# Layer 2 of a four-layer model: the gated branch's last batch placed beside the collecting of the experts' rows

## The chip, the core and the metric

The kernel runs on one core of a Trainium2 chip. The metric is the device time of one execution in microseconds (us), lower is better. The engines of the core are PE (matrix products and transposes), DVE (vector work), ACT (activations and copies), POOL (here it issues the indirect transfers) and SP (it issues the plain transfers). Each engine works through its own queue in order, and they meet through semaphores. A "window" below is a stretch of the profiled span, and "clock" is the share of full speed that the throttle granted to PE.

## What is computed

The model has four layers on `x` of 4 batches of 1024 tokens of 128 numbers (float32). Every layer takes a layer norm of `x` and adds two branches of it to `x`. Only layer 2 and its borders matter here:

```python
xn = _layernorm(x)
x  = x + _L2_attn_ref(xn, ...) + _L2_ffn_ref(xn, ...)

# _L2_attn_ref: the gated branch, for each batch by itself; S=128, E=256
xn   = x / max(norm(x) * D**-0.5, EPS) * g
uv   = silu(xn @ uv_w.T);  u, v, base = uv[:E], uv[E:2E], uv[2E:]   # along the last axis
q, k = rope(base * gamma + beta)
kern = square(relu((q @ k.T + w_rel[idx]) / sqrt(S)))
out  = x * res_scale + (u * (kern @ v)) @ o_w.T

# _L2_ffn_ref: eight experts, top 2 of each token, 640 rows for an expert
probs      = softmax(xf @ router_w.T);  topw, topi = top_k(probs, 2)
# tokens sorted by expert and by falling weight; those ranked past 640 are dropped
eo         = (silu(disp @ wg) * (disp @ wu)) @ wd                   # disp: the rows of each expert
out[token] += eo[expert, rank] * weight
```

## The kernel before

`x` and `xn` lie on chip as 128 channels by 4096 tokens, in eight tiles of 512 tokens (`NT`, `W`). Layer 2 (`_layer2`, L1736) has three stages.

**Stage A** runs two generators against each other under an order written out by hand (`manual_schedule` for PE, DVE, ACT and POOL): the routing (`_dispatch`) and the gated branch (`_gated`, L1568). `_layer2` takes one step of the routing after each step of the gated branch, and two after each of the first eight. Whatever a generator issues between two of its `yield`s stands together in the engines' queues.

The routing turns `xn` to rows of tokens, `xtok` (four PE transposes L909 and an ACT copy L910 for each of the eight tiles), computes the logits (L918, 32 products into the PSUM tile `lg`), softmax and top two on DVE (L930 to L965), and then finds for each expert the weight of its 640th heaviest token: `_heaviest` searches it bit by bit from bit 29 to 0. For a bit DVE counts (L868), PE sums the counts over partitions (L873), DVE sets the bit and the next candidate (L874 to L877). Ranks, slots and addresses follow (to L992), and then POOL issues 64 scatters (L1000), each of 128 token rows of `xtok` into the experts' buffer `buf` in memory. They all write one buffer, and each waits for the one before.

The gated branch runs over four batches. For a batch `project` normalises (L1611, L1612), makes `u`, base and `v` (L1621, L1634, activations on ACT) and turns the base (`gy`, L1649, L1657, L1660 on DVE). Then, for two halves of the queries and eight blocks of keys, `score` makes a product (L1666, near the diagonal one more, L1670), ACT adds the relative weight (L1672), DVE squares (L1674, `gkern`), and `weigh` (L1681) multiplies by `v` into the accumulator `gacc`, two products for a block. After eight blocks DVE multiplies by `u` (L1690), and `close` (L1695, L1700, L1701) projects back and adds to `x`. The scores of the next half, and the projection of the next batch (`ahead`), are issued between the weighings. A float32 product of 512 columns shows as two matmuls in the profile.

**Stage B** (`_experts`, L1007): SP loads an expert's weights (L1020 to L1022) and its rows from `buf` (L1027), PE and the others compute, SP stores the outcome to `res`.

**Stage C** takes `_collect` and `_norm_beside` by turns (`_together`), in an order that the scheduler chooses. `_collect` has, for each of the eight tiles, eight gathers by POOL (L1081, 128 rows each), DVE's weighing of the rows (`cl_y`, L1089, L1091), four PE transposes (L1092, into the PSUM tile `cl_tp`), and an addition to `x` (L1094). Six row buffers of each kind let the gathers run ahead. `_norm_beside` is the layer norm of layer 3 behind it: centring (L286, L287, ACT square L289), variance (L306 to L312) one tile behind, scaling (ACT L317, PE L320, DVE L321) two tiles behind. The first products of layer 3 (convolutions L1793, activations L1801, stores of rows to memory L1802, betas L1814 and L1815) follow and use `xn` as its tiles come out; the last of those four stores, for batch 3, is used below as the end of stage C.

Layer 0 uses `_dispatch` without the search, and `_collect` beside its shared expert (`_shared`, L1112 to L1117).

Of the kernel before, what the change touches and what calls it, by code (L numbers as in the profile page):

```python
# [11 lines left out]
F32 = mybir.dt.float32  # L12
# [6 lines left out]
PSUM = bass.MemoryType.PSUM  # L19
DRAM = bass.MemoryType.DRAM  # L20

P = 128
B, L, D = 4, 1024, 128
T = B * L
W = 512
NT = T // W
# [263 lines left out]
    return sq  # L290


def _norm_beside(k, whole):


    nc, tc = k.nc, k.tc
    with tc.tile_pool(name="nb", bufs=3) as w, tc.tile_pool(
        name="nb_ps", bufs=2 if whole else 1, space=PSUM
    ) as misc:
        squares = {}  # L300

        def variance(t):
            st = misc.tile([P, W], F32, name="misc")
            sq, own = squares.pop(t), slice(4 * t, 4 * t + 4)
            for i in range(4):
                nc.tensor.matmul(  # L306
                    st[:, i : i + 1], sq[:, i * P : (i + 1) * P], k.mean[:, 0:1], start=True, stop=True
                )
            nc.vector.tensor_copy(k.var[:, own], st[:, :4])
            if whole:  # L310
                nc.scalar.activation(k.inv[:, own], k.var[:, own], AF.Sqrt, bias=k.eps5)
                nc.vector.reciprocal(k.inv[:, own], k.inv[:, own])  # L312

        def scale(t):
            c = slice(t * W, (t + 1) * W)
            spread = w.tile([P, 4, P], F32, name="nb_s")
            nc.scalar.copy(spread, _bc(k.inv[:, 4 * t : 4 * t + 4], 2, P))  # L317
            ps = misc.tile([P, W], F32, name="misc")
            for i in range(4):
                nc.tensor.transpose(ps[:, i * P : (i + 1) * P], spread[:, i], k.ident)  # L320
            nc.vector.tensor_tensor(k.xn[:, c], k.xn[:, c], ps, ALU.mult)  # L321

        for t in range(NT + 2):
            if whole and t >= 2:
                scale(t - 2)
            if 1 <= t <= NT:
                variance(t - 1)
            if t < NT:
                squares[t] = _centre(k, t, misc, w)
            if t < NT:  # L330
                yield
# [509 lines left out]
    return a  # L841


def _heaviest(k, weight, pool):


    nc = k.nc
    flat = lambda t: t.rearrange("p t e -> p (t e)")
    by_expert = lambda t: t.rearrange("p t e -> p e t")

    def turned(src):

        ps = k.misc.tile([P, W], F32, name="misc")
        for m in range(2):
            nc.tensor.transpose(ps[:, m * P : (m + 1) * P], src[:, m * P : (m + 1) * P], k.ident)
        return ps[:, : 2 * P]


    row = pool.tile([P, 2 * P], F32, name="bis_row")
    mask = pool.tile([P, 2 * P], F32, name="bis_mask")  # L860
    nc.vector.tensor_copy(row, turned(flat(weight)))
    part = pool.tile([P, 1], F32, name="bis_part")

    thr, cand, on = (pool.tile([P, 1], I32, name="bis_" + n) for n in ("thr", "cand", "on"))
    nc.vector.memset(thr, 0)
    nc.vector.memset(cand, 1 << 29)
    for bit in range(29, -1, -1):
        nc.vector.tensor_scalar(  # L868
            mask, row, cand.bitcast(F32), None, ALU.is_ge, ALU.add, accum_out=part
        )  # L870
        yield
        ps = k.misc.tile([P, W], F32, name="misc")
        nc.tensor.matmul(ps[:, :1], k.same8, part, start=True, stop=True)  # L873
        nc.vector.tensor_scalar(on, ps[:, :1], float(CAP), float(1 << bit), ALU.is_ge, ALU.mult)  # L874
        nc.vector.tensor_tensor(thr, thr, on, ALU.bitwise_or)
        if bit:
            nc.vector.tensor_scalar(cand, thr, 1 << (bit - 1), None, ALU.bitwise_or)  # L877
    equal, above = (pool.tile([P, TT, E], F32, name="bis_" + n) for n in ("equal", "above"))
    for dst, op in ((above, ALU.is_gt), (equal, ALU.is_equal)):
        nc.vector.tensor_scalar(mask, row, thr.bitcast(F32), None, op)  # L880
        yield
        nc.vector.tensor_copy(flat(dst), turned(mask))
    left, n = (pool.tile([P, E], F32, name="bis_" + n) for n in ("left", "n"))
    nc.vector.tensor_reduce(n, by_expert(above), AX.X, ALU.add)
    yield
    ps = k.misc.tile([P, W], F32, name="misc")
    nc.tensor.matmul(ps[:, :E], k.ones, n, start=True, stop=True)
    nc.vector.tensor_scalar(left, ps[:, :E], -1.0, float(CAP), ALU.mult, ALU.add)
    rank = _prefix(k, equal, pool, "bis_rank")
    nc.vector.tensor_tensor(rank, rank, _bc(left, 1, TT), ALU.is_lt)  # L890
    nc.vector.tensor_tensor(equal, equal, rank, ALU.mult)
    nc.vector.tensor_tensor(equal, equal, above, ALU.add)
    return equal


def _dispatch(k, rw, normed, by_weight, den_eps, keep, rows, bufs, banks, got):
# [3 lines left out]
    with tc.tile_pool(name="rt", bufs=1) as r, tc.tile_pool(name="rtw", bufs=2) as w, tc.tile_pool(  # L900
# [1 line left out]
    ) as k.misc, tc.tile_pool(name="rt_lg", bufs=1, space=PSUM) as lp:  # L902

        xtok = rows.tile([P, TT, D], F32, name="xtok")
        for t in range(NT):
            ps = k.misc.tile([P, W], F32, name="misc")
            for i in range(4):
                c = t * W + i * P
                nc.tensor.transpose(ps[:, i * P : (i + 1) * P], k.xn[:, c : c + P], k.ident)  # L909
            nc.scalar.copy(xtok[:, 4 * t : 4 * t + 4, :].rearrange("p t d -> p (t d)"), ps)  # L910
            yield

        lg = lp.tile([P, TT, E], F32, name="lg")
        for t in range(NT):
            c = slice(t * W, (t + 1) * W)
            x = k.xn[:, c]
# [44 lines left out]
        if by_weight:  # L961
            nc.vector.tensor_tensor(pr, hot[0], _bc(top[0], 2, E), ALU.mult)
            nc.vector.tensor_tensor(tmp, hot[1], _bc(top[1], 2, E), ALU.mult)
            nc.vector.tensor_tensor(pr, pr, tmp, ALU.add)
            nc.vector.scalar_tensor_tensor(pr, chosen, -1.0, pr, ALU.add, ALU.add)  # L965
            chosen = yield from _heaviest(k, pr, r)
            yield
            rank = _prefix(k, chosen, r, "rank")
            kept = chosen
        else:  # L970
            rank = _prefix(k, chosen, r, "rank")
            kept = r.tile([P, TT, E], F32, name="kept")
            nc.vector.tensor_scalar(kept, rank, float(CAP), None, ALU.is_lt)
# [95 lines left out]
def _collect(k, got, res, acc, banks):  # L1069


    nc, tc = k.nc, k.tc
    with tc.tile_pool(name="cl", bufs=6) as g, tc.tile_pool(name="cl_ps", bufs=banks, space=PSUM) as ps:
        for t in range(NT):
            tp = ps.tile([P, W], F32, name="cl_tp")
            for i in range(4):
# [56 lines left out]
def _layer0(k, a):  # L1133
    _layer_norm(k)
    with k.tc.tile_pool(name="keep0", bufs=1) as keep:
        rw = k.load(keep, a["l0_rw"])
        with k.tc.tile_pool(name="rows0", bufs=1) as rows:
            got = []
            for _ in _dispatch(k, rw, True, False, 0.0, keep, rows, [k.buf[0]] * 2, 4, got):
                pass  # L1140
            _attention0(k, a)
        _experts(k, a["l0_rg"], a["l0_ru"], a["l0_rd"], k.buf[:1], k.res[0])
        _together(_shared(k, a, k.x), _collect(k, got, k.res[0], k.x, 1), _norm_beside(k, False))

# [418 lines left out]

def _gated(k, a):  # L1568


    nc, tc = k.nc, k.tc
# [1 line left out]
    with ExitStack() as s:  # L1573
# [22 lines left out]
        def project(z):  # L1596
# [18 lines left out]
            for half in range(2):  # L1615
                own = slice(half * W, (half + 1) * W)
                for dst, at in ((base, 512), (z.u, 0)):
                    yield
                    ps = big.tile([P, 2, W], F32, name="big")
                    for m in range(2):  # L1620
                        nc.tensor.matmul(  # L1621
                            ps[:, m, :],
                            uvw[:, at + m * P : at + (m + 1) * P],
# [53 lines left out]
        def weigh(z, half, jc):  # L1677
            if jc == 0:
                z.acc = accs.tile([P, 2, W], F32, name="gacc")
            for e in range(2):  # L1680
                nc.tensor.matmul(  # L1681
                    z.acc[:, e, :],
                    z.v[:, jc, e * P : (e + 1) * P],
# [16 lines left out]
            nc.vector.scalar_tensor_tensor(t, k.xn[:, c], k.vec("l2_rs"), ps, ALU.mult, ALU.add)  # L1700
            nc.vector.tensor_tensor(k.x[:, c], k.x[:, c], t, ALU.add)  # L1701

        zs = [SimpleNamespace(b=b, kern=([], [])) for b in range(B)]
        for _ in project(zs[0]):
            yield
        for jc in range(8):
            yield
            score(zs[0], 0, jc)
        ahead = iter(())
        for n in range(2 * B):  # L1710
            z, half = zs[n // 2], n % 2
            if half == 0 and n // 2 + 1 < B:
                ahead = project(zs[n // 2 + 1])
            for jc in range(8):
                yield
                if n + 1 < 2 * B:
                    if jc == 0 and half == 1:
                        for _ in ahead:
                            pass
# [1 line left out]
                    if half == 0:  # L1721
                        next(ahead, None)
                    yield
                weigh(z, half, jc)
                if jc == 2 and n:
                    close(zs[(n - 1) // 2], (n - 1) % 2)
                if half == 0:
                    next(ahead, None)
                    if jc % 2:
                        next(ahead, None)  # L1730
        yield
        close(zs[-1], 1)
        yield


def _layer2(k, a):  # L1736
    _layer_norm(k)
    with k.tc.tile_pool(name="keep2", bufs=1) as keep:
# [2 lines left out]
        got = []  # L1741
        with k.tc.tile_pool(name="rows2", bufs=1) as rows, k.tc.manual_schedule(engines=ENGINES3):
            routes = _dispatch(k, rw, False, True, 1e-6, keep, rows, k.buf[1:] * 2, 1, got)
            gated = _gated(k, a)
            next(gated)
            for n, _ in enumerate(gated):
                next(routes, None)
# [2 lines left out]
            for _ in routes:  # L1750
                pass
        _experts(k, a["l2_rg"], a["l2_ru"], a["l2_rd"], k.buf[1:], k.res[1])
        _together(_collect(k, got, k.res[1], k.x, 2), _norm_beside(k, True))

# [533 lines left out]
```

## Time and profile before

| | us |
|---|---|
| median of 3 runs (lowest, highest) | 4741.51 (4738.85, 4744.04) |
| the profiled execution | 4741.99 |
| its span | 4740.2 |
| layer 2: last logits end | 3470.27 |
| layer 2: search | 3484.4 to 3560.5 |
| layer 2: scatters, first start and last end | 3581.91, 3747.60 |
| layer 2: rows of the first expert reach PE | 3763.13 |
| layer 2: first gather | 3888.79 |
| layer 3: store of the rows of batch 3 | 3998.10 |

The moments count from the start of the span. The granted clock over the span is 0.859. PE is busy for 83% of the span, DVE for 65%, ACT for 54% and POOL for 14%; such shares are means over stages with different limits, so what bounds layer 2 has to be read in its own windows. In a row of the windows the first figures are the length and then, for each engine, its busy time and its number of instructions. A row of the waits gives the engine and line that waited, what it waited for, the sum, the number and the longest. In the timeline the bracket at the end is the idle time before the instruction and what ended it.

### The profile page before, as it was taken

The numbers are of one execution on the slowest core, as the hardware profiler recorded it, in microseconds if no ns is written. First come the engines' busy times: TensorE is split into PE (matmuls) and PEld (weight loads), VectorE is DVE, ScalarE is ACT, GpSimd is POOL, SyncE is SP. The second block draws the span as 40 slices with busy tenths as digits, with TensorE's granted clock in tenths as the row PEclk, the third lists the DMA queues.
The fourth block names the chain that finished last, engine by engine and source line by source line (L and its number), as shares of the span: only waits on it lengthen the run. The fifth ranks groups of instructions, "written<-read, shape, count | busy, mean of one in ns | idle before, by whom it ended". The sixth has DMA issues, their size and how long they took to land. (4 is left out here: it accounts for less than half of the span.)

```text
span 4740.2 us, 54727 instructions
## 1 busy us (share of the span) xinstructions
PE 3911.8 (83%) x21048; PEld 1791.9 (38%) x21048; DVE 3093.1 (65%) x4481; ACT 2583.1 (54%) x3674; POOL 685.3 (14%) x632
## 2 busy tenths in 40 slices
PE   4679999998968888888886888888879986898675
PEld 3223333364422222222223555555544463343221
DVE  5868989722335655656567888888565323799686
ACT  1257877831249999999993555555422222343332
POOL 2310000003200000000003223233103213000242
PEclk6689999999977777767777999999889997999688
DMA  2411111021221010010002111111100122400001
GB/s 87 119 41 56 29 56 29 11 70 50 15 83 58 18 50 18 27 36 18 18 1 78 34 36 41 36 37 34 51 1 20 52 72 67 109 1 9 0 0 53
DMA packets 107496, 191.83 MB, mean 40 GB/s; under 512 B 23138, under 2 KB 48354, under 8 KB 105378
## 3 DMA queue, kind: packets, MB, share of 16 engines
q1 hardware_dynamic: 98756, 166.31, 12.4%
q0 software_dynamic: 8192, 16.79, 1.7%
q10 hardware_dynamic: 288, 5.24, 0.3%
q8 instruction: 166, 2.72, 0.2%
q14 instruction: 94, 0.77, 0.1%
HBM read 95.00 MB, written 67.39 MB: 34 GB/s over the span
## 5 line engine op out<-in xcount | busy, mean ns | idle before, releaser
L790 DVE TENSOR_TENSOR p<-p,e 128x1024 f32<-128x1024 f32 x512 | 586.4, 1219 | 322.0 <-ACT e L788 322.0
L773 PE MATMUL big<-q,k 32*128 32x512 f32 x2048 | 559.3, 631 | 181.8 <-ACT p L784 76.7
L583 DVE TENSOR_REDUCE m<-mx 128x2 f32<-128x1024 f32 x512 | 620.9, 1223 | 101.2 <-PE mx L575 94.1
L468 PE MATMUL av<-p,v 128*32 128x256 f32 (+1 forms) x5632 | 666.3, 528 | 0.2
L666 ACT ACTIVATE p<-s 128x512 f32<-128x512 f32 x1024 | 551.1, 597 | 187.9 <-PE s L657 174.4
L773 PEld LDWEIGHTS big<-q,k 32*128 32x128 f32 x2048 | 210.0, 228 | 706.4 <-ACT e L788 351.1
L657 PE MATMUL s<-q,k 64*128 64x512 f32 x1024 | 278.6, 496 | 45.7 <-DMA q<-mrows 31.3
L788 ACT ACTIVATE e<-big,neg_mu 128x1024 f32<-128x1024 f32 x256 | 262.2, 1126 | 12.5 <-PE big L773 12.3
L575 PE MATMUL mx<-k,q 64*128 64x512 f32 x1024 | 239.4, 438 | 32.4 <-DVE m L583 17.8
L784 ACT ACTIVATE p<-big,neg_mu 128x1024 f32<-128x1024 f32 x256 | 261.3, 1201 | 2.5 <-PE big L773 2.3
L788 ACT ACTIVATE e<-big 128x1024 f32<-128x1024 f32 x256 | 242.6, 1040 | 27.5 <-PE big L773 25.9
L784 ACT ACTIVATE p<-big 128x1024 f32<-128x1024 f32 x256 | 239.4, 1072 | 8.4 <-PE big L773 8.1
L1227 POOL TENSOR_TENSOR lqk<-lt 128x512 f32<-128x512 f32 x128 | 162.7, 1271 | 516.5 <-DVE lt L1218 450.3
L1081 POOL DMA_INDIRECT cl_row<-res,back x128 | 122.3, 955 | 727.8 <-DMA in_l_su_sb<-in_l_su 473.5
L1200 PE MATMUL lps<-f_wqkv,lh 128*128 128x512 f32 x384 | 215.4, 649 | 11.0 <-DVE lo L1355 6.8
L468 PEld LDWEIGHTS av<-p,v 128*32 128x32 f32 x5632 | 121.3, 111 | 254.8 <-issue 205.2
L657 PEld LDWEIGHTS s<-q,k 64*128 64x128 f32 x1024 | 107.9, 184 | 284.2 <-issue 161.1
L1318 ACT ACTIVATE lsm<-lsm 128x512 f32<-128x512 f32 x128 | 80.6, 630 | 222.0 <-DVE lsm L1317 220.5
L1000 POOL DMA_INDIRECT buf<-xtok,to x128 | 129.0, 1008 | 402.5 <-DMA buf<-xtok,to 222.5
L1193 POOL MEMSET lva<- 128x32 f32 x16 | 2.4, 152 | 1147.0 <-PE av L468 1147.0
L1049 DVE TENSOR_TENSOR h<-h,up 128x640 f32<-128x640 f32 x64 | 52.6, 821 | 159.9 <-PE up L1046 80.7
L575 PEld LDWEIGHTS mx<-k,q 64*128 64x128 f32 x1024 | 108.5, 195 | 62.9 <-DVE m L583 46.8
(427 smaller groups left out, 7043.3 us busy)
## 6 DMA issues: line engine op xcount, KB each, us to landing
hl<-phi SPq DMA_DIRECT2D x64, 256.0 KB
hl<-plo SPq DMA_DIRECT2D x64, 256.0 KB
lvs<-lva SPq DMA_DIRECT2D x16, 520.0 KB
q<-hl SPq DMA_DIRECT2D x32, 256.0 KB
k<-hl SPq DMA_DIRECT2D x32, 256.0 KB
q<-hl SPq DMA_DIRECT2D x16, 512.0 KB
k<-hl SPq DMA_DIRECT2D x16, 512.0 KB
lvs<-lva SPq DMA_DIRECT2D x16, 390.0 KB
```

The source lines that it names most:

```text
L468: k.nc.tensor.matmul(av[32 * j : 32 * j + 32, cols], v[:, kc, 9 * (4 * g + j) : 9 * (4 * g + j) + 32], pts[j][:, cols], start=kc == 0, sto ...
L575: nc.tensor.matmul(ps[:, i, :], q[rows, gg, qt * P : (qt + 1) * P], key[rows, gg, half * W : (half + 1) * W], start=True, stop=True, tile_ ...
L583: nc.vector.tensor_reduce(m[:, qt, gg, :, half], ps, AX.X, ALU.max)
L657: nc.tensor.matmul(ps, key[rows, half, kc * P : (kc + 1) * P], q[rows, half, qh * W : (qh + 1) * W], start=True, stop=True, tile_position= ...
L666: nc.scalar.activation(p, ps, AF.Exp, scale=8.0**-0.5)
L773: nc.tensor.matmul(ps[:, jj, :], key[rows, kc * P : (kc + 1) * P], q[rows, qh * W : (qh + 1) * W], start=True, stop=True, tile_position=(3 ...
L784: nc.scalar.activation(p, ps, f, bias=bias, scale=scale)
L788: nc.scalar.activation(e, ps, f, bias=bias, scale=scale)
L790: nc.vector.tensor_tensor(p, p, e, ALU.mult)
L1000: nc.gpsimd.indirect_dma_start(out=buf, out_offset=bass.IndirectOffsetOnAxis(ap=to[:, t : t + 1], axis=0), in_=xtok[:, t, :], in_offset=None,)
L1200: nc.tensor.matmul(ps, z.h[:, t * P : (t + 1) * P], wqkv[:, own], start=True, stop=True)
L1227: nc.gpsimd.tensor_tensor(z.qk[t][:, own], r[0], r[1], ALU.add)
```

## The change

The gated branch takes the list of its batches. In stage A it runs batches 0 to 2; batch 3 runs in stage C, step by step beside the collecting and the norm, under an order written by hand. Its weights and tables are loaded and its unit variance computed a second time there. In the routing with search, `xtok` is no longer made ahead of the logits: one tile of it is issued behind PE's product of each of the first eight bits, in a PSUM tile of the logits' pool. Two products that stood together (in `project` for `u` and base, and in `weigh`) get a `yield` between them, and the steps of the projection ahead move accordingly. `_collect` gets eight row buffers of each kind instead of six (in layer 0 too), and in layer 2 one PSUM bank for its transposes and one for the norm instead of two each.

```diff
-def _norm_beside(k, whole):
+def _norm_beside(k, whole, banks):
...
-        name="nb_ps", bufs=2 if whole else 1, space=PSUM
+        name="nb_ps", bufs=banks, space=PSUM
...
-def _heaviest(k, weight, pool):
+def _heaviest(k, weight, pool, beside):
...
         nc.tensor.matmul(ps[:, :1], k.same8, part, start=True, stop=True)
+        for fn in itertools.islice(beside, 1):
+            fn()
         nc.vector.tensor_scalar(on, ps[:, :1], float(CAP), float(1 << bit), ALU.is_ge, ALU.mult)
...
         xtok = rows.tile([P, TT, D], F32, name="xtok")
-        for t in range(NT):
-            ps = k.misc.tile([P, W], F32, name="misc")
+
+        def take(ps, t):
             for i in range(4):
                 c = t * W + i * P
                 nc.tensor.transpose(ps[:, i * P : (i + 1) * P], k.xn[:, c : c + P], k.ident)
             nc.scalar.copy(xtok[:, 4 * t : 4 * t + 4, :].rearrange("p t d -> p (t d)"), ps)
-            yield
-
-        lg = lp.tile([P, TT, E], F32, name="lg")
+
+        if not by_weight:
+            for t in range(NT):
+                take(k.misc.tile([P, W], F32, name="misc"), t)
+                yield
+
+        logits = lambda: lp.tile([P, W], F32, name="lg")
+        lg = logits()[:, : TT * E].rearrange("p (t e) -> p t e", e=E)
...
-            chosen = yield from _heaviest(k, pr, r)
+
+            beside = iter([lambda t=t: take(logits(), t) for t in range(NT)])
+            chosen = yield from _heaviest(k, pr, r, beside)
...
-    with tc.tile_pool(name="cl", bufs=6) as g, tc.tile_pool(name="cl_ps", bufs=banks, space=PSUM) as ps:
+    with tc.tile_pool(name="cl", bufs=8) as g, tc.tile_pool(name="cl_ps", bufs=banks, space=PSUM) as ps:
...
-def _gated(k, a):
+def _gated(k, a, batches):
...
                     for m in range(2):
+                        if m:
+                            yield
                         nc.tensor.matmul(
                             ps[:, m, :],
...
             for e in range(2):
+                if e:
+                    yield
                 nc.tensor.matmul(
                     z.acc[:, e, :],
...
-        zs = [SimpleNamespace(b=b, kern=([], [])) for b in range(B)]
+        zs = [SimpleNamespace(b=b, kern=([], [])) for b in batches]
...
-        for n in range(2 * B):
+        for n in range(2 * len(zs)):
             z, half = zs[n // 2], n % 2
-            if half == 0 and n // 2 + 1 < B:
+            if half == 0 and n // 2 + 1 < len(zs):
                 ahead = project(zs[n // 2 + 1])
...
                     if half == 0:
                         next(ahead, None)
                     yield
-                weigh(z, half, jc)
+                if half == 0 and jc % 2 == 0:
+                    next(ahead, None)
+                yield from weigh(z, half, jc)
                 if jc == 2 and n:
                     close(zs[(n - 1) // 2], (n - 1) % 2)
                 if half == 0:
                     next(ahead, None)
-                    if jc % 2:
-                        next(ahead, None)
         yield
         close(zs[-1], 1)
-        yield
+        yield True
...
-            gated = _gated(k, a)
+            gated = _gated(k, a, range(B - 1))
...
-        _together(_collect(k, got, k.res[1], k.x, 2), _norm_beside(k, True))
+
+        with k.tc.manual_schedule(engines=ENGINES3):
+            gated, collect = _gated(k, a, [B - 1]), _collect(k, got, k.res[1], k.x, 1)
+            norm = _norm_beside(k, True, 1)
+            next(gated)
+            for t in range(NT):
+                next(collect)
+                if t < NT - 2:
+                    next(norm)
+                for _ in range(8):
+                    if next(gated):
+                        raise ValueError("the branch ends ahead of the collecting")
+            while not next(gated):
+                pass
+            for g in (norm, norm, norm, collect, gated):
+                next(g, None)
```

More of the change, by code (lines that the diff above doesn't have):

```diff
@@ L1142, in _layer0 @@
         _experts(k, a["l0_rg"], a["l0_ru"], a["l0_rd"], k.buf[:1], k.res[0])
-        _together(_shared(k, a, k.x), _collect(k, got, k.res[0], k.x, 1), _norm_beside(k, False))
+        _together(_shared(k, a, k.x), _collect(k, got, k.res[0], k.x, 1), _norm_beside(k, False, 1))
 class _Slots:
@@ L1715, in _gated @@
                 yield
-                if n + 1 < 2 * B:
+                if n + 1 < 2 * len(zs):
                     if jc == 0 and half == 1:
```

## The prediction

> **What bounds the kernel now.** All times are microseconds from the start of the profiled span. I first read the windows of layer 2, then the waits and queue timelines of its two halves, last the chain of waits. The columns of the windows are length, then busy time and count of PE, weight loads, DVE, ACT and POOL, then granted clock, DMA share and GB/s.
>
> ```profile
> span 4740.2 us, 54727 instructions
> 3484.00:3520.00 36.00, 26.53 (x71) 14.29 (x72) 28.16 (x106) 8.21 (x13) 0.00 (x0) 0.68 0.00 1
> 3640.00:3680.00 40.00, 38.63 (x99) 17.64 (x98) 13.99 (x20) 11.95 (x17) 15.65 (x16) 1.00 0.07 25
> 3720.00:3757.00 37.00, 35.22 (x82) 15.12 (x80) 9.37 (x13) 4.72 (x7) 11.32 (x11) 1.00 0.20 63
> 3885.00:3910.00 25.00, 5.91 (x15) 2.86 (x15) 5.86 (x17) 1.91 (x2) 16.30 (x17) 0.58 0.24 55
> 3950.00:3970.00 20.00, 6.01 (x18) 3.61 (x18) 4.09 (x12) 1.25 (x2) 13.16 (x14) 0.51 0.25 49
> 3970.00:3990.00 20.00, 16.65 (x67) 9.60 (x67) 11.64 (x36) 12.14 (x18) 5.75 (x6) 0.89 0.17 46
> ```
>
> The first half (stage A: routing, search and scatters beside the gated branch) has PE full at clock 1.00 after the search. The collecting (stage C) has PE a quarter to a third busy at clock 0.50 to 0.66 until its end, with POOL issuing gathers. So the change moves PE work from a full stretch to an empty one.
>
> ```profile
> 3581.91 1.07 POOL L1000 DMA_INDIRECT buf<-xtok,to  x1 [140.66 <-DVE slot L982]
> POOL buf L1000 <- DMA buf<-xtok,to: 97.5, 62, 2.9
> 3746.63 0.97 POOL L1000 DMA_INDIRECT buf<-xtok,to  x1 [1.54 <-DMA buf<-xtok,to]
> 3749.02 0.33 SPq L1020 DMA_DIRECT2D g_w<-in_l_rg  x1
> 3757.94 1.97 PE misc L1695 x4
> 3759.97 3.03 DMA rows<-buf
> ```
>
> The 64 scatters run from 3581.91 to 3747.60, 2.51 apart, each behind the landing of the one before: 165.7 in all. SP's load of the experts' weights follows 1.4 after the last. But `rows<-buf` leaves only at 3759.97, behind the last close (L1695) and its addition. The gated branch ends stage A, and scatters alone would have ended it some 9.4 earlier.
>
> ```profile
> POOL cl_row L1081 <- issue: 156.4, 51, 141.2
> DVE xn L321 <- remote: 20.6, 2, 13.1
> DVE var L309 <- remote: 9.5, 2, 4.9
> DVE x L1094 <- remote: 3.9, 1, 3.9
> 3918.84 13.07 another core or an unknown queue
> 3957.44 7.52 another core or an unknown queue
> ```
>
> Stage C runs from the first gather, 3888.79, to layer 3's last store of row b3 at 3998.10: 109.3. The gathers take 0.955 and a gap of 0.30, so 64 need 81. The rest is a chain through DVE and PE, with odd holes: DVE waits although the product it needs has ended on PE. The semaphore records show that PE's update comes 1 to 10.7 after the matmul's end, in some 30 of 381 signalling matmuls near gathers, never over 0.06 among 4,570 elsewhere. The chain calls it an unknown queue; "remote" sums to 34.0, 0.53 per gather.
>
> **Part 1: the search comes sooner.** Layer 2's eight xtok transposes and copies leave the head of the queue and go one to a search bit. The last logits end at 3470.27 before. By the queues' order of the changed kernel they end near 3453, and 9.1 to 13.6 of DVE work follow (row L930 to L861, 13.6 before): bis_row near 3466, 17 to 18 earlier. The 30 bits took 3484.4 to 3560.5, 2.45 each on average, though the first seven took 1.98. Split products let a bit's small matmul (L873) wait for half a pair, 0.86, not 1.72. I count 8 early bits with gated work at the slow clock between them, 21.75; 18 at 1.98, 35.7; 4 under scores, 9: 66.5. So the threshold comes near 3532.6. Slots and the way to the first scatter took 3560.7 to 3581.9, 21.2. First scatter near 3554.0, **27.9 earlier**; at 2.45 per bit still, 21.
>
> **Part 2: the gated branch shrinks.** One batch is, by the trace's 0.43 per pass: scores L1666/L1670 36 passes 15.5, weighs L1681 64 passes 27.5, big L1621 16 passes 6.9, closes L1695 8 passes 3.4, v L1634 about 3.4, transposes 1: 57.7. Three batches after the search need 3 x 57.7 less what fits into the search, about 150, and overhead of 17 as before (19 on 179): end near 3699. The scatters' end, 3554.0 + 165.7 = 3719.7, is later, so scatters now bound stage A with a cover of 20. The experts' rows then come 1.4 + 1.3 + some 4 behind, 3726.5, against 3763.13: **-36.6**; I give back 1.6 for a colder PE at the experts' start: **-35**. Without the earlier search it would be -9.4.
>
> **Part 3: the last batch in stage C.** New there: loads of uv, ow, rot2 and near again (2.0 MB, five issues on SP, ahead of layer 3's stores; the first loading of them ran among 4.0 MB at up to 415 GB/s, so 5 to 6 or hidden), the unit variance again, and 57.7 of PE work, written in rounds: collecting of tile t, norm of a tile, eight gated steps. PE, DVE and ACT are in-order, so a late row (2.76 after issue) holds cl_y on DVE, and behind it gated's gy, gkern, gx; these hold PE's scores. Before, the scheduler chose the order freely; now each round is a loop of 8 cl_y (2.5), add 0.69, centre, variance, scale and back to PE. The bank of cl_tp is 1, not 2, and gated's big has 1. Rounds by PE: 0.9+5.2, 3.4, 3.4, 7.7, 7.7, 6.9, 6.9, then 12 with 3.4 of closes, plus 3 to 4 for collect and norm each, plus the hand-overs (ACT 0.6, DVE 0.69 each way): 12 to 13 per round against 10.1 for eight gathers. Last close near g0 + 117 (g0 the first gather). The tail of norm of the last two tiles, and layer 3's first products that no longer fill holes, 18.5 where it was 14.7 (3983.42 to 3998.10). So 135.6 against 109.3: **+26**. If rounds keep the gathers' pace: 82.6 + 19.4 (half of the last tile's weighs and closes) + 18.5 = 120.5, **+11**: the lower bound.
>
> **Part 4: late updates of PE.** The 64 gathers remain, and PE has several times as many products that ACT and DVE wait for. Bounds: 0 (all under other work; in layer 0, where gathers come in bursts of eight beside a full PE, PE was 60.00 of 60.00 busy) to 41.6 (all the blocked stretches before, exposed again). In layer 0's dense first burst of 24 gathers PE lost 13.8 of 40 (26.21 busy), 0.57 per gather, so density counts. Rounds of 12.5 stand for a density of 0.8; I take half of 64 x 0.53: **+17**.
>
> The Trainium skill, "SBUF — State Buffer", section "SBUF: two separate sides", speaks against such a charge: the ports of the engines and of DMA are apart, so a transfer cannot slow a computing engine. It names one trap, VectorE keeping GpSimd from writing descriptors. The trace differs: in the 13.07 hole gathers went on every 1.26 while DVE stood. By the page the term would be 0 and the sum 17 lower.
>
> **Part 5: small terms.** The clock: PE 60 to 75% busy, rows between 0.5 and 0.9; a pass takes 0.43 at clock 1.00 and two passes of L286 took 2.07 at half, so 57.7 of passes could grow by 0 to +20 where PE is the bound of a round; **+3**, since the moved work itself raises the clock. Eight row buffers for six: 16 gathers ahead for 12; in layer 0 the dense burst grows (8 x 0.57 = 4.6 at most, later bursts shrink), -2 to +5, **+2**. Table loads of 1.283, between silu and square root, 0 to +5, inside the 26.
>
> Sum: 4741.99 - 35 + 26 + 17 + 3 + 2 = **4755**. The profiled run is 0.48 above the median shown, 4741.51: no correction.
>
> **The rivals.** (a) *Faster: the gathers stay the clock of stage C.* Rounds fit in 10.1, late updates fall under the gated products: -35 + 11, with 0 to 5 of rest: 4718 to 4723. For it: layer 0's full PE beside gathers; PE 12.24 of 20 at most busy until the end. It decides if POOL never waits for cl_y over 1 after the first buffers. Against: in-order DVE and ACT pass every hold on.
> (b) *Cancel:* rounds of 12.5, but no late update exposed: -35 + 26 + 3: 4736.
> (c) *Much slower:* all late updates exposed (+41.6) and a clock of 0.6 (+10 to 20): 4785 to 4800. The dense burst of layer 0 speaks for it, the low density in longer rounds against it.
> (d) *The scatters do not come sooner as said:* the search stays paced by the PE products between bits (2.45 and more), gain 15 to 25 not 35: it adds 10 to 20 to each case, mostly to mine.
>
> **How the numbers follow.** Chances: forecast (4742 to 4780) 0.48, (a) 0.25, (b) 0.18, (c) 0.09; (d) lies in the forecast's upper part. A measurement tells 0.2%, 9.5, from no change, so faster is below 4732, slower above 4751. Faster: (a). Same: (b) less 0.03 below 4732, and 0.05 of the forecast. Slower: the rest. Its own range is 4742 to 4780; with (a) and (b) it reaches from 4714, 4780 above leaves out most of (c).
>
> **What would show it.** First scatter near 3554 (27.9 earlier), last near 3719, `rows<-buf` within 7 of the last scatter, not behind L1695: parts 1 and 2. In stage C: POOL waiting for cl_y in each round (rounds near 12.5), PE 55 to 75% busy, first gather to b3's store 150 to 160. "Remote" waits of DVE and ACT of 15 to 20 show part 4; near 0 with rounds of 10 shows (a). The prediction is wrong if stage A's end moves by under 20, if stage C takes under 125, or if layer 0 moves by over 5.

## The result, and the profile after

The changed kernel takes 4797.71 us (median of 4, 4796.71 to 4802.50) against 4742.77 for the kernel before beside it: ratio 1.0117, interval 1.0100 to 1.0135. It is 55 slower. The forecast was 4755 with a range to 4780: the right side, but 43 short.

The profiled execution of the changed kernel:

```profile
span 4796.4 us, 54727 instructions
```

Cut at moments that both traces have (start of layer 0's collecting, end of its shared expert's last product into `sgp`, first scatter of layer 2, first gather, first product of the betas, end), the 56.2 between the two spans divide like this:

| stretch | before | after | difference | forecast |
|---|---|---|---|---|
| up to layer 0's first gather | 1112.6 | 1111.4 | -1.2 | 0 |
| layer 0's collecting beside the shared expert | 204.7 | 213.7 | +9.0 | +2 |
| layer 1, routing and search, to the first scatter | 2264.6 | 2246.0 | -18.6 | -28 |
| scatters and experts, to the first gather | 306.9 | 298.4 | -8.5 | -7 (-35 + 27.9) |
| stage C, first gather to the first product of the betas | 108.6 | 185.5 | +76.9 | +46 (26 + 17 + 3) |
| the rest | 742.8 | 741.4 | -1.4 | 0 |

Of the -18.6 layer 1 took +6.6, which no other execution shows again (4.9 at most, b4n), and the earlier search gave -25.2. Stages A and B came close. Stage A's end first. These are rows of the timeline of the changed kernel (start, length, engine, line, operation, the idle time before in brackets):

```profile
3571.14 1.06 POOL L1010 DMA_INDIRECT buf<-xtok,to  x1 [115.26 <-DVE slot L992]
3718.06 1.96 PE L1709 MATMUL misc<-gprod,in_l_ow_sb 128*128 128x512 f32 x4 [1.41 <-DVE gprod L1704]
3736.63 0.97 POOL L1010 DMA_INDIRECT buf<-xtok,to  x1 [1.53 <-DMA buf<-xtok,to]
3744.96 1.30 PE L1045 MATMUL rows_ps<-in_const_sb,rows 128*128 128x128 f32 x5 [24.94 <-DMA rows<-buf]
```

The gated branch's last product of stage A ends at 3720.0, the last scatter at 3737.6. The scatters set the end, with a cover of 17.6 (forecast 20), and the experts' rows reach PE 7.4 behind them.

Stage C is where the time went. Its windows (length, busy time of PE, weight loads, DVE, ACT, POOL, then granted clock, DMA share, GB/s) and its waits, changed kernel:

```profile
3880.00:3900.00 20.00, 11.93 (x21) 4.83 (x21) 6.85 (x17) 3.44 (x4) 15.12 (x17) 0.59 0.36 58
3900.00:3920.00 20.00, 10.75 (x23) 5.14 (x23) 4.00 (x9) 5.54 (x6) 7.37 (x8) 0.67 0.13 30
3940.00:3960.00 20.00, 16.17 (x37) 7.59 (x37) 10.81 (x25) 6.83 (x11) 8.05 (x9) 0.74 0.14 26
4000.00:4020.00 20.00, 18.60 (x46) 7.81 (x44) 6.25 (x14) 1.19 (x2) 0.00 (x0) 1.00 0.00 0
```

```profile
POOL cl_row L1091 <- DVE cl_y L1099: 40.2, 8, 14.8
PE cl_tp L1102 <- DVE cl_y L1101: 30.1, 21, 13.8
DVE x L1104 <- remote: 19.8, 1, 19.8
ACT gu L1640 <- remote: 8.8, 1, 8.8
```

Three things are to be seen. First, under the 32 gathers that eight row buffers allow (3869.5 to 3909.5), PE is half busy and hand-overs from PE are late ("remote"): DVE's addition of the second tile waits 19.8. Second, when that is over the rounds do not fall to 12 or 13. POOL, which now waits for a free row buffer in every round, starts its eight gathers at 3924.30, 3940.92, 3959.57 and 3977.89: rounds of 16.6, 18.7 and 18.3, with PE some 80% busy at a clock of 0.74 to 0.80 (3940 to 3980). One whole round on PE:

```profile
3959.74 0.33 PE L1102 MATMUL cl_tp<-in_const_sb,cl_y 128*128 128x128 f32 x1 [1.14 <-DVE cl_y L1101]
...
3961.76 1.04 PE L320 MATMUL misc<-in_const_sb,nb_s 128*128 128x128 f32 x4
3963.58 1.87 PE L306 MATMUL misc<-mean,sq 128*128 128x1 f32 x8 [0.78 <-issue]
3965.70 2.07 PE L286 MATMUL misc<-x,mean 128*128 128x512 f32 x2 [0.26 <-issue]
3967.57 1.53 PE L1695 MATMUL gacc<-gkern,gv 128*128 128x512 f32 x2
...
3978.06 0.33 PE L1102 MATMUL cl_tp<-in_const_sb,cl_y 128*128 128x128 f32 x1 [2.09 <-DVE cl_y L1101]
```

From one first transpose to the next it is 18.3: transposes with gaps 2.0, scaling and the wait for the norm's one bank 1.8, variance and a second such wait 2.1, centring 1.9, then the gated products 8.4 (3967.57 to 3975.97), then 2.1 in which PE waits for DVE's `cl_y`. DVE is in order, and the last `gkern` of the round, itself behind PE's last score and ACT, stands ahead of it. The trace gives both waits for the bank to no releaser ("issue"), but DVE's readings of it end at 3963.52 and 3965.64, 0.06 before PE goes on. Everything but the gated products is 9.9, and nothing of it lies under them: collecting and norm stand as one block at the head of the round. That block also runs at half the clock:

```profile
3964.00:3967.00 3.00, 2.75 (x9) 2.14 (x10) 0.34 (x2) 0.30 (x1) 2.20 (x3) 0.50 0.21 48
3967.00:3970.00 3.00, 3.00 (x6) 1.24 (x6) 0.69 (x1) 0.63 (x1) 1.91 (x2) 0.73 0.20 44
3970.00:3973.00 3.00, 3.00 (x8) 1.33 (x7) 0.69 (x1) 0.60 (x1) 0.00 (x0) 1.00 0.13 22
```

The variance's products take 1.87 here; before, 0.95 for the tiles whose products stood behind convolutions (at 3945.32 and 3975.21). The granted clock in the trace is 0.5 from 3961.77 to 3968.59, then 1.0 until 3978.83: it doubles 2.9 after PE's last gap (0.26, before 3965.70), and the rounds that begin near 3924, 3941 and 3978 have such a stretch of 0.5 too. The Trainium skill, "TensorE: Matmul & The Clock Gate", section "Part 1: The HAM clock gate", says the gate opens only after some 3.4 us of steady work; the rows agree roughly.

Third, the end is longer. The gated branch's last product ends at 4023.30, 153.8 behind the first gather, and layer 3's first convolution stands right behind it:

```profile
4021.35 1.95 PE L1709 MATMUL misc<-gprod,in_l_ow_sb 128*128 128x512 f32 x4 [1.41 <-DVE gprod L1704]
4023.58 2.74 PE L1822 MATMUL qh<-xn,tap_w 128*128 128x512 f32 x6
```

From there to the store of batch 3's rows (4055.74) it is 32, where the forecast had 18.5. Before, the convolutions began at 3932.68, 45 ahead of the last gather.

### The profile page after: what moved, and what is told of

It reads as the page before. It is cut to its first block, busy times and chain, and to the rows that moved or that the text cites. A ratio compares the mean times of both kernels' runs of the same rounds, so it can differ in the third digit from the quotient of the medians.

```text
span 4796.4 us, 54727 instructions
## 1 busy us (share of the span) xinstructions
PE 3942.5 (82%) x21048; PEld 1809.4 (38%) x21048; DVE 3097.4 (65%) x4486; ACT 2582.8 (54%) x3675; POOL 681.8 (14%) x632
```

## The experiments

All ratios are against the kernel before on the same chip. A column that no expectation foresaw turned out to matter: on the chips of some runs (those of the two kernels above, of a6, a4, b8 and b4, and of a8f, a4n and a4fk) updates of PE's semaphore come late while gathers stream ("late updates" below); on those of the other eight kernels not one of them was over 0.1 us late. The kernel before took 4742.77, 4746.80 and 4743.61 on the former, 4722.66 and 4722.92 on the latter. Each chip served at one time only, so no run tells whether it is the chip or the time that differs.

| kernel | ratio | interval | late updates | layer 0 | stage C |
|---|---|---|---|---|---|
| before (six buffers) | 1 | | yes | 204.7 | 108.6 |
| after (eight, by hand) | 1.0117 | 1.0100 to 1.0135 | yes | 213.7 | 185.5 |
| a6 | 1.0079 | 1.0061 to 1.0097 | yes | 204.9 | 182.8 |
| a4 | 1.0047 | 1.0030 to 1.0064 | yes | 196.2 | 173.2 |
| b8 | 1.0029 | 1.0018 to 1.0041 | yes | 214.5 | 114.6 |
| b4 | 0.9978 | 0.9968 to 0.9987 | yes | 196.4 | 108.2 |
| c_sp | 1.0083 | 1.0063 to 1.0104 | no | 196.6 | 162.8 (from the loads) |
| a4s | 1.0050 | 1.0031 to 1.0068 | no | 189.6 | 153.0 |
| p1 | 1.0028 | 1.0016 to 1.0039 | no | 195.3 | 98.9 |
| b2 | 1.0036 | 1.0021 to 1.0050 | no | 209.8 | 98.8 |
| after2 (the changed kernel) | 1.0085 | 1.0069 to 1.0102 | no | 197.5 | 173.6 |
| a4f | 1.0005 | 0.9995 to 1.0014 | no | 189.7 | 132.4 |
| a4k | 1.0036 | 1.0023 to 1.0048 | no | 189.7 | 147.6 |
| b4n | 0.9988 | 0.9978 to 0.9998 | no | 189.6 | 97.9 |
| a8f | 1.0046 | 1.0029 to 1.0063 | yes | 214.7 | 166.2 |
| a4n | 1.0043 | 1.0026 to 1.0060 | yes | 191.7 | 173.6 |
| a4fk | 0.9993 | 0.9984 to 1.0003 | yes | 193.0 | 146.7 |

Layer 0 is the stretch from its first gather to the end of the shared expert's last product into `sgp`, stage C that from the first gather to the first product of the betas, both in one profiled execution of each kernel. In a4 and a4n updates come late in layer 0 alone (three and two of them, by 4.2 at most).

### The row buffers: a6, a4, b8, b4

```diff
-    with tc.tile_pool(name="cl", bufs=8) as g, ...   # after
+    with tc.tile_pool(name="cl", bufs=6) as g, ...   # a6; 4: a4
-    with tc.tile_pool(name="cl", bufs=6) as g, ...   # before
+    with tc.tile_pool(name="cl", bufs=8) as g, ...   # b8; 4: b4
```

> The changed kernel with six row buffers again instead of eight. Theory A (PE's semaphore updates come late while gathers stream densely, so the number of gathers that can run ahead sets the loss): layer 0's first burst goes from 32 to 24 gathers and gives back its 8; stage C's dead stretch after the first gather (40 of it under 32 gathers) gets shorter by 8 to 10; total 4775 to 4785. Theory B (the cost is the hand-written rounds with single banks, and layer 0's and 1's 15 are drift of one execution): total 4792 to 4800.

> The changed kernel with four row buffers: eight gathers ahead, one round. Theory A: layer 0's first burst is 16, 14 to 18 less than with eight buffers; stage C's first burst is 16 and its dead stretch 20 shorter, while later rounds may wait for rows by up to 2 each: total 4755 to 4775. Theory B: 4790 to 4800, or slower by waits for rows.

> The kernel before with eight row buffers, nothing else. Theory A: layer 0 loses 8 (burst of 32), what follows it in layer 1 shows whether the further 6.6 belong to it; stage C hardly changes since its gathers stream all through: total +6 to +16. Theory B: within 0.2% of before.

> The kernel before with four row buffers. Theory A: layer 0 gains 4 to 8 (burst of 16); stage C has shorter bursts, fewer late updates, but gathers wait for rows: -10 to +10 there; total -15 to +5. Theory B: layer 0 unchanged, stage C slower by 0 to 10: total 0 to +10.

Medians: a6 4783.20, a4 4768.84, b8 4760.27, b4 4737.38. All four went as theory A said for layer 0. The eight buffers alone make the old kernel 13.5 slower (4760.27 against 4746.80; 6.1 of it in stage C, where hardly a change was expected), four alone make it 9.4 faster. Layer 0 takes 196, 205 and 214 with four, six and eight buffers, whose first dense bursts are 16, 24 and 32 gathers: 9 for each eight gathers more, almost the 10.1 that eight gathers last. PE does not stand still in a burst, but works at about half its pace on these chips: with eight buffers (b8) 46 of the shared expert's matmuls end in the first 50, later some 20 in every 10. Not all of it is late updates: without them layer 0 still takes 189.7 with four, 195.3 with six and 197.5 with eight (runs below); why is open. In the changed kernel's stage C the step from eight to four gives 12.3 (185.5 to 173.2), much less than the 77: theory A does not carry it. The 6.6 by which layer 1 was longer in the changed kernel's execution did not come back in b8 (0.4): it belongs to that execution.

### The gathers taken out of stage C: c_sp

```diff
-                    nc.gpsimd.indirect_dma_start(out=row, ..., in_=res, in_offset=...)
+                    nc.sync.dma_start(row, res[n * P : (n + 1) * P, :])   # layer 2 alone
```

The rows are then not those that the tokens need; the selection of rows is left out.

> The changed kernel, with layer 2's 64 gathers replaced by plain loads of the same size that SP issues (the rows are then not those that the tokens need: the selection of rows is left out). No gather streams in stage C any more. Theory A (late updates of PE carry stage C's cost, 185 from the first gather to the betas against 109 before): no late update, rounds of 12 to 13, stage C near 135, total near 4745. Theory B (the rounds' own hand-overs and half-speed products carry it): only the dead stretch under the first burst goes, 20 to 25, rounds stay at 16 to 18, stage C near 160, total near 4772.

Stage C, counted from the issue of its loads, is 162.8 where it was 186.2, and the rounds are 18.9, 18.3 and 17.1 without any gather (first transposes at 3902.83, 3921.70, 3939.99 and 3957.05, behind waits of 2.96, 1.14, 2.09 and 0.43 for `cl_y`). That is theory B: 23 went, the rounds stayed. The run fell on a chip without late updates, so it does not tell whether the 23 were theirs. After2, the changed kernel on such a chip, needs 174.3 from its loads: so 12 of the 23 came with the chip, and 11 with the gathers themselves. After2's rounds, with gathers and no late update, are 17.0, 19.0 and 18.4.

### Collecting and norm spread over the round: a4s

```diff
-            tp = ps.tile([P, W], F32, name="cl_tp")     # _collect: the four y first, then
+            yield                                       # a step, then the transposes
...
             if whole and t >= 2:
                 scale(t - 2)
+            yield
             if 1 <= t <= NT:
                 variance(t - 1)
+            yield
...
-                next(collect); next(norm); 8 x next(gated)
+                for step in (collect, gated, collect, gated, norm, gated, gated, norm, gated, gated, norm, gated, gated):
+                    next(step)
```

> The changed kernel with four row buffers, and in stage C the collecting's transposes and the norm's three parts (scaling, variance, centring) each put between two gated steps instead of in one block at the head of a round. Same work, same banks. Theory B: the waits for the single bank and for DVE fall under gated products and PE stays warm, rounds of 16.5 to 18.5 become 13 to 14, 20 to 30 less than the kernel with four buffers: 4740 to 4750. Theory A: rounds do not change by more than 1 each: 4762 to 4770.

Rounds on PE with the same work and the same banks (timeline of a4s):

```profile
3901.39 3.10 PE L1690 MATMUL misc<-gqk,gqk 128*128 128x512 f32 x4
3904.33 0.95 PE L306 MATMUL misc<-mean,sq 128*128 128x1 f32 x8
3905.14 1.96 PE L1690 MATMUL misc<-gqk,gqk 128*128 128x512 f32 x4
3906.94 1.02 PE L286 MATMUL misc<-x,mean 128*128 128x512 f32 x2
```

The waits for the norm's bank are gone, and the variance takes 0.95, the centring 1.02: full clock. POOL's eights start at 3869.07, 3881.89, 3895.99, 3911.56, 3926.42 and 3938.28, 13.8 on the mean. Stage C is 153.0, against 173.2 and 173.6 with the same four buffers in a4 and a4n, where no update came late in stage C either, and 173.6 in after2. So 20 of the cost were where the steps stood in PE's queue: the last gated product ends 122.5 behind the first gather, in a4 142.6. What follows it, to the first product of the betas, stays at 30.5 (a4 30.6). It is still 0.5% slower than before: shorter rounds, but the branch's rest and the last norms come behind the last gather, 51 where the old kernel has 20.

### The earlier search alone: p1

```diff
-            gated = _gated(k, a, range(B - 1))
+            gated = _gated(k, a, range(B))
-        with k.tc.manual_schedule(engines=ENGINES3):   # the whole of stage C
+        _together(_collect(k, got, k.res[1], k.x, 2), _norm_beside(k, True, 2))   # and six buffers
```

> Only the earlier search, the tokens' rows beside it and the split products: all four batches stay in stage A, stage C and the six buffers as before. By the prediction's part 2 the gated branch's end, not the scatters, sets stage A's end: first scatter about 25 earlier, stage A's end 0 to 5 earlier, total -5 to +3 against before. If instead the scatters bound it, total -20 to -30.

A miss: 4736.48 against 4722.66, not about 0 but 14 slower. The timeline of SP in p1:

```profile
3725.66 0.33 SPq L1030 DMA_DIRECT2D g_w<-in_l_rg  x1
3767.43 4.90 SPq L1037 DMA_DIRECT2D rows<-buf  x3
```

The weights follow the last scatter at 3725.66, and the rows follow the gated branch 41.8 later. Counted from layer 1's last store the search is as early as in the changed kernel (first scatter at 531.0, as in most executions of the changed order; before 551.6), but the branch ends 13 later than before: its first score starts 13.5 later (480.7 against 467.2), because the routing's DVE work, softmax to eighth bit, now stands ahead of the branch's first `gy`. The new order does not make stage A shorter by itself; it takes 13 from the branch and gives 20 to the routing. It pays only when the branch has been shortened, and in the changed kernel it has: its cover of 17.6 has this in it.

### Two buffers in layer 0: b2

```diff
-        _together(_shared(k, a, k.x), _collect(k, got, k.res[0], k.x, 1), _norm_beside(k, False))
+        _together(_shared(k, a, k.x), _collect(k, got, k.res[0], k.x, 1, 2), _norm_beside(k, False))   # 2 for 6
```

> The kernel before with two row buffers in layer 0 alone (four gathers ahead), six in layer 2. If each gather of the dense first burst costs layer 0's PE some 1.2, as 8 to 6 to 4 buffers showed (about 10 for eight gathers), the burst of 8 saves 16 to 20 against six buffers: total -14 to -20. If rows then come late for layer 0's additions: no gain over four buffers (-9), or slower.

14 slower: the expectation's second case, late rows, and worse than the -9 that it thought of first. Layer 0 takes 209.8 where six buffers take 195.3 on chips without late updates. Four gathers ahead are too few: DVE's first weighing of a tile now waits for rows eight times, 15.4 in all (3.9 in four waits in p1).

### The changed kernel again, free order, tables kept: after2, a4f, a4k, b4n

```diff
-        with k.tc.manual_schedule(engines=ENGINES3):    # stage C; a4f, from a4
+        if True:
...
-        uvw, ow, rot, near, norm: loaded or computed anew by each _gated     # a4k, from a4s
+        uvw, ow, rot, near, norm: made in stage A, kept in the layer's pool
-        two times four gated steps in each of eight rounds
+        ten gated steps in each of the first seven rounds
```

> The changed kernel itself, on the chip of the other three, to tell what the chip does: in the last four kernels no update of PE came late at all, in the first four they did as in the kernel before. If late updates are there: as at first, +55 against before, 186 from the loads of stage C to the betas. If they are not: layer 0 gives back some 17, the dead stretch in stage C 20 or so, the rounds of 18 stay: +35 to +42 against before.

> The changed kernel with four row buffers, and stage C without the order by hand: the scheduler puts the gated steps, collecting, norm and layer 3's first products in its own order, as it did before the change. Theory B (blocks at the head of a round cost the time): rounds melt, 15 to 25 less in stage C than with four buffers and the order by hand (174): 150 to 160. Theory C (PE's work itself, 115 warm, with any order): stage C 165 to 175.

> The kernel with the norm's parts spread (stage C 154 without late updates), and further the gated branch's tables kept on chip from stage A instead of loaded again, and ten gated steps in each of the first seven rounds, none in the eighth. The first product of uv no longer waits for its load (14 at the start of stage C with PE almost idle), and the branch ends before the last collecting: 12 to 20 less, stage C 135 to 142 without late updates, 145 to 155 with them; against before +0 to +8.

> The kernel before with four row buffers, again, on the chip of these kernels. With late updates: -9 as at first (ratio 0.998). Without: layer 0's first burst costs less, -3 to -6.

After2 is the changed kernel without an edit, and it is 42 slower than before (4764.96 against 4722.92), as expected without late updates. ACT's waits for PE in the first round show the difference, first the changed kernel on the chip of the prediction, then after2:

```profile
3905.41 1.02 ACT L1640 ACTIVATE gu<-big 128x1024 f32<-128x1024 f32 x1 [8.79 <-remote]
```

```profile
3882.86 1.02 ACT L1640 ACTIVATE gu<-big 128x1024 f32<-128x1024 f32 x1 [2.07 <-PE big L1633]
```

The same activation, behind the same four products, waits 2.07 for them where the update comes at once, and 8.79 on the other chip, 5.1 of these after the product's end (3900.26).

A4f is the largest single step: 4724.57, level with the kernel before, and 40 less than after2. Of the 48 between the two profiled spans (4769.5 and 4721.3) 8 are layer 0's buffers (197.5 to 189.7) and 41 stage C (173.6 to 132.4). Theory B's number was 150 to 160, so the free order did even better. Two of its windows:

```profile
3900.00:3920.00 20.00, 18.25 (x57) 9.08 (x56) 13.07 (x34) 7.40 (x13) 12.76 (x13) 0.91 0.22 42
3940.00:3960.00 20.00, 19.38 (x52) 9.07 (x51) 4.90 (x9) 0.92 (x2) 0.00 (x0) 1.00 0.00 0
```

PE is 91 to 97% busy here at a clock of 0.91 to 1.00 (from 3860 to 3900 it was 79% at 0.75 to 0.84), and POOL waits over 2 only once (2.62) for a row buffer after the first gather. The last gated product ends 111.0 behind the first gather, and what follows, to the first product of the betas, takes 21.4. Layer 3's convolutions fill no holes here either: the first starts at 3959.0, behind the branch's last product (3958.3). The gain lies in the order of the branch, the collecting and the norm.

A4k missed: 147.6, not 135 to 142, and 14.6 above the kernel before, not 0 to 8. Without the loads PE's first 20 of stage C are still little used (5.66 busy); that the first rows, which stand ahead of the branch in the order by hand, hold it is likely but not shown. B4n held: four buffers gain some 6 without late updates (0.9988).

### On one chip: the order alone, the buffers alone, the reload: a8f, a4n, a4fk

```diff
-        with k.tc.manual_schedule(engines=ENGINES3):    # stage C; a8f, from the changed kernel
+        if True:
```

A4n is a4 without an edit; a4fk is a4f with the tables kept as in a4k.

> The changed kernel with one edit: stage C without the order by hand. If the order by hand is the main cause in itself, whatever the buffers: 25 to 40 less than the changed kernel, +0.1 to +0.4% against before without late updates, +0.5 to +0.7% with them. If the free order needed the four buffers (through layer 0): less than 20.

> The changed kernel with four row buffers and the order by hand, beside the one with the free order and eight. Without late updates the buffers matter in layer 0 alone: 5 to 8 less than the changed kernel, +0.7% against before; with them +0.5%, as at first.

> Free order, four buffers, and the gated branch's tables and norms kept on chip from stage A. If the loads at the start of stage C hold PE (5 of 20 busy in its first window with the free order), it is 6 to 12 less than the same with the loads, which stood at +0.05% of before: -0.1 to -0.2% against before, stage C near 124 instead of 132. If the first rows hold it anyway (the first transposes can't start sooner than 10 after the first gather): no change.

Medians 4770.13, 4764.46 and 4739.88 beside 4743.61; this chip has late updates. By the ratios the free order alone takes 0.7% from the changed kernel, which ran on another such chip (1.0117 to 1.0046, a little better than the 0.5 to 0.7% over before that was expected with late updates), and the four buffers alone as much (a4n, 1.0043, mostly layer 0). Order and burst are two causes. In a8f's profiled execution stage C goes from 185.5 to 166.2 only, half of the 41 without late updates and with four buffers, but that execution is 12.9 above its kernel's median. In its window from 3910 to 3930 PE is 4.90 of 20 busy, amid 45 gathers with hardly a gap. A4fk, which has neither the eight buffers, nor the order by hand, nor the reload, is within noise of before (0.9993; -0.1 to -0.2% was expected). Its stage C is 146.7, not 124: PE does 13.09 in the first 20, but only 5.57 in the next, and updates come late in its stage C too. How much keeping the tables would gain without late updates was not run.

B4 is the one version that beat both kernels, on both kinds of chip: 0.9978 and 0.9988, from one number.

## Why the prediction was wrong

**What held.** The direction; that the scatters would set stage A's end, with a cover near 20 (17.6); the way from the last scatter to the first gather (-8.5 against -7); the search's length (66.1 in most executions of the new order, 61.8 in the profiled one, forecast 66.5, before 76.1); that late updates exist and cost more in longer bursts; and POOL waiting for `cl_y` in each round.

**Part 1** was too generous by 7. The last logits end 8.8 sooner after layer 1's last store (431.2 against 440.0, in a6, a4, a4f and p1), not 17: the first logit does start 14 sooner, but the 32 products now take 17, not 12. With the shorter way to the search the first scatter comes 20.7 sooner in most executions (25.2 in the profiled one), not 27.9. The working's lower bound, 21, came out by luck: it stood for slower bits, and the bits were as forecast; the logits were late.

**Part 3 is the step that failed**, in two terms: "12 to 13 per round", and the 18.5 behind the last close.

The rounds first. The gated products of a round were right (7.7 forecast for the middle rounds, 8.4 measured). But with 3 to 4 each for collecting and norm and the hand-overs, the prediction's own terms add up to 15 and more for such a round; to come to 12 or 13, a part had to be hidden under the gated products, and nothing was. Collecting and norm stand in one block in PE's queue, measured 9.9 of 18.3 with three things that were not in the sum: the single bank's waits (1.0), the 2.1 for `cl_y` behind the last `gkern`, and half clock for variance and centring (3.7 where a4s has 2.0; part 5 had 3 for the clock in all of stage C). Without late updates (after2) the last gated product ends 141.8 behind the first gather, where 117 and 3 for the clock were forecast. The runs that show it: after2 and c_sp (rounds of 17 to 19 without late updates, and without gathers), a4s (13.8 and 122.5 with the steps spread) and a4f (111.0 with the order freed).

The end second. The prediction saw that layer 3's products would no longer fill holes, and charged 18.5; it is 32 in the changed kernel (31.7 to the first product of the betas; after2 31.8). In the order by hand the norm's last steps stand behind the whole branch too. Spreading the rounds does not shorten this (30.5 in a4s), the free order does (21.4 in a4f).

**Part 4** had the right mechanism, and its size was near: 12 of stage C (185.5 against 173.6 for the changed kernel on the two kinds of chip), forecast 17. It missed something else: whether updates come late at all depends on the chip. One reading was off: the 10.7 of the latest update is counted from a later product than the one that DVE waited for; it is 14.2 (last section).

**Part 5** named layer 0's buffers and took +2 from a range up to +5. They cost 9 (b8 10), 1.1 to 1.2 for each of eight gathers instead of 0.57. Without late updates eight buffers instead of six cost 2 there (197.5 against 195.3), as forecast; what was missed is that the late updates grow with the burst.

Together: 31 of stage C, 7 of layer 0 and 9 of the way to the first scatter (in the profiled execution mostly layer 1's 6.6, in the others the search) make 47; the scatters, the start and the rest gave back 4. The 31 of stage C are 22 for the rounds and 14 for the end, less 5 that part 4 had too much.

Of the rivals, (c) had the right time, 4785 to 4800, for a wrong reason: it charged late updates of 41.6 and a slow clock over the whole stage. The clock was part of it (0.74 to 0.80), but through the blocks.

## What to carry to other kernels

When steps are interleaved by hand on in-order queues, add up each engine's queue for one round with every wait, and take nothing as hidden that stands in one block: what is hidden has to stand between other work in that very queue. Freeing the order, or spreading the steps, is worth a run before the idea is given up; here the same move of work cost 75 in blocks and 35 in the scheduler's order, on chips of one kind. A deeper prefetch is no free edit: two more row buffers made a stage slower that did not need them, since they let the gathers come in a longer burst.

## What the runs showed of the hardware

Semaphore updates of PE come late while POOL's gathers stream every 1.26, on the chips of eight of the profiled kernels here besides the one before, and never by over 0.1 on those of the other eight; the changed kernel was on both kinds. The longest hole of the kernel before:

```profile
3916.68 1.06 PE L320 MATMUL misc<-in_const_sb,nb_s 128*128 128x128 f32 x4
3919.34 1.87 PE L306 MATMUL misc<-mean,sq 128*128 128x1 f32 x8 [1.60 <-ACT sq L289]
3931.93 0.69 DVE L321 TENSOR_TENSOR xn<-xn,misc 128x512 f32<-128x512 f32 x1 [13.09 <-remote]
```

DVE waits for the product that ended at 3917.74; its update is recorded at 3931.91, 14.2 later. PE itself had gone on to its next products meanwhile. The updates come in clumps: in the changed kernel those of products that ended at 3910.27, 3910.48, 3910.69, 3910.80, 3910.91 and 3911.70 arrive between 3913.07 and 3913.98. (The profile's ends of products are modelled, so a lateness is as good as the model; on the chips without late updates it is 0.1 at most.) Away from gathers none was over 0.2 late on any chip, scatters included, each of which waits for the landing of the one before (2.51 apart at the median). The Trainium skill, "SBUF — State Buffer", section "SBUF: two separate sides", keeps transfers and engines apart; for eight of the kernels here its rule held, for the others the hand-over was slowed, while in the rows above PE's own work went on. What makes a chip one or the other stays open.

The difference between such chips is 20 to 24 for the kernel before, 0.4 to 0.5%, more than many a tuning step: only ratios on one chip can be compared.
